# A two-layer transformer on one core: order of two readers of a PSUM bank, key sums, elu minimum, slot numbers and shifts of the plan changed together

## The chip, the cores and the metric

The kernel runs on one core of a Trainium2 chip. A core has a matrix engine (TensorE, here PE, with its weight loads listed apart as PEld), a vector engine (VectorE, DVE), a scalar engine (ScalarE, ACT), a general engine (GpSimd, POOL) and a queue that issues transfers (SyncE, SP). Each has its own stream of instructions, and they meet through semaphores. SBUF is the working memory; PSUM, in eight banks of 128 x 512 numbers here, takes the output of PE, and DVE and ACT read it. The metric is the device time of one execution in microseconds (us); all numbers are float32.

## The reference, cut to what matters

The input is 16 sequences of 256 tokens of width 128. Four blocks follow each other, each with a residual and a LayerNorm:

```python
x = _layernorm(x + L0_attn(x))   # 16 heads of 64, softmax over 256 keys
x = _layernorm(x + L0_ffn(x))    # each token picks one of 64 small splines
x = _layernorm(x + L1_attn(x))   # linear attention and a 65-wide window attention, mixed by a gate
x = _layernorm(x + L1_ffn(x))    # causal attention with normed q and k, then 8 experts of 512
```

Two pieces are touched by the change. In L1_attn the linear attention is

```python
q = jax.nn.elu(q) + 1.0
k = jax.nn.elu(k) + 1.0
kv = jnp.einsum('bsd,bse->bde', k, v)
num = jnp.einsum('bsd,bde->bse', q, kv)
denom = jnp.einsum('bsd,bd->bs', q, k.sum(axis=1))
return num / (denom[..., None] + 1e-06)
```

In L1_ffn the attention divides q and k of each head by their length, `x / sqrt(sum(x * x) + eps)`, before the scores, with 16 heads of 64 and a causal mask over the 256 tokens of a sequence.

## The kernel before, in words

**Groups and stages.** The 4096 tokens are cut into 8 groups of 512 (two sequences, four tiles of 128 tokens). Each group goes through five stages: A (`stage_a`, L773) the first attention, B (`stage_b`, L896) the splines, C (`stage_c`, L1011) linear and window attention, D (`stage_d`, L1241) the causal attention and the gate of the experts, E (`stage_e`, L1398) the experts. Stage D of one group runs while A of a later one and E of an earlier one do, so that PE is fed from several stages.

**The plan.** No stage issues instructions by itself. Each calls `W.add` (L133) with the engine or engines allowed ("VS" is DVE or ACT), a cost in ns, what it reads and writes, a due number, and buffers it must hold. A dependency between two tasks arises only where one of them writes; two readers of the same PSUM buffer are free of each other in the plan. `Plan.order` (L176) takes the due numbers, which are the group's number plus the stage's offset `OFF` (L39) and a fraction within the stage, and adds the random shifts that follow from the seeds in `SHIFTS` (L108). `Plan.line` (L199) then builds one list: again and again it takes the task that could start first by the planned costs, latencies (`LAG`, `OWN`), a price for a change of PE's tiling mode (`DRAIN`, `CHANGE`) and for a change of ACT's function table (`SWITCH`). The engine of a "VS" task, and the slot of each buffer, are settled there too. The list is issued as it stands, so every engine works off its part strictly in that order. Semaphores are put in by the framework afterwards. It also keeps two engines from reading one PSUM bank at once: whichever reader stands second in the list waits for the first, although the plan knows of no such order.

**Slots.** `SLOTS` (L41) gives each class of buffers its number: `ua` (q, k, v of stage A), `uq` and `ud` (q; k and v of stage D), `pb` and `pt` (weights of a softmax before and after transposing), `ov` (attention output), `m`, `k1` (small ones), `c` (stage C), `h2` (stage E's input) and `e` (its sum), and so on. PSUM has four single banks `p` and two double ones `s`.

**The chain of a pair of heads.** `pair` (L635) is used by A and D. PE makes scores into `s`; DVE takes the maximum (L684, or L665 to L680 in D); ACT makes the exponentials and their sums (L703); DVE takes the reciprocal (L710); POOL scales (L716); PE transposes (L731); DVE or ACT copies to `pt` (L583 or L581); PE multiplies by v, and the result is copied to `ov`.

**Ahead of the pairs in D** (`half`, L1251), per half of a sequence's heads: PE projects q into a bank `ps_q`. ACT squares it into `sq` (L1276), and two halves of the same bank are scaled into `uq` by DVE or ACT (L1286 or L1284). PE adds the squares over each head (`hsum`, at L575). k is projected likewise: ACT squares (L1314), DVE or ACT copies the bank to `kn` (L583 or L581), DVE adds the squares (L1318). `rsqrt` (L1225) is a chain of twelve small DVE instructions that ends at L1239. POOL scales `kn` (L1333), PE transposes it (L1343), and the copy `ud` feeds the scores.

**Linear attention in C.** PE projects q into a bank; one reader adds a bias into `ql` (L1031, ACT or DVE), a second one on DVE takes the minimum for elu into `el` (L1032) from the same bank. `outer` (L1065) makes k-transposed times v for a batch with two matmuls of 128 columns, and then the sums of k with two matmuls against a column of ones, `ones1`. The 129 columns are copied to `kv`, and `numer` multiplies q by them.

**The experts in E** (L1398): per expert PE makes four matmuls of 512 columns (`p<-h,w`), ACT a gelu each (L1427), PE sixteen of 128 (`p<-w,hid`), DVE adds with the gate (L1443).

Of the kernel before, what the change touches and what calls it, by code (L numbers as in the profile page):

```python
# [36 lines left out]
NBURST = 2  # L37

OFF = {"a": 0.0, "b": 1.0, "c": 2.0, "d": 3.0, "e": 4.0}  # L39

SLOTS = (  # L41
    ("x", 512, 5),
    ("xT", 512, 1),
    ("ua", 512, 6),
    ("uq", 512, 3),
    ("ud", 512, 5),
    ("pb", 512, 4),
    ("pt", 512, 4),
    ("ov", 256, 7),
    ("m", 64, 30),  # L50
    ("k1", 256, 5),
    ("b", 512, 2),
    ("sc", 288, 1),
    ("c", 512, 7),
    ("qm", 512, 1),
    ("pbC", 512, 3),
    ("ptC", 512, 2),
    ("d", 512, 3),
    ("h2", 512, 2),
    ("kn", 512, 2),  # L60
    ("sq", 512, 2),
    ("e", 512, 2),
    ("hid", 512, 6),
    ("w1", 512, 2),
    ("w2", 512, 2),
# [28 lines left out]
class Plan:  # L94
# [11 lines left out]


    SHIFTS = (  # L108
        258498, 374385, 681190, 1030615, 451157, 416595, 399254, 90386, 402651, 32248, 805286, 535455, 818580,
        975896, 569904, 458668, 418336, 881271, 734960, 774165, 174958, 721137, 512294, 399542, 597858, 678718,  # L110
        303725, 282346, 639604, 797258, 109727, 890232, 734346, 822941, 513168, 691104, 300099, 248650, 750519,
        73556, 12134, 849073, 440403, 472645, 90759, 219759, 480546, 47153, 162702, 851150, 655540, 189313,
        520359, 246779, 231756, 3563, 719028, 365367, 228824, 1016760, 1007179, 536322, 391257, 681015, 841744,
        764356, 292336, 874227, 260578, 294584, 597654, 539960, 432998, 981216, 157434, 356760, 634378, 612323,
        725626, 1029404, 668235, 831714, 603426, 765582, 703452, 266006, 294902, 137908, 1000104, 774373,
        483527, 143664, 261087, 128566, 532895, 360314, 43841, 427189, 701184, 612361, 280258, 1039547, 958460,
        806151, 268661, 680903, 1021345, 131940, 609221, 510023, 159915, 864272, 945906, 103959, 945224,
        853953, 102848, 251619, 243385, 34464, 1011407, 809975, 279597, 61512, 283715, 625865, 369054, 760197,
        54915, 795619, 988242, 350995, 1010712, 973541, 85859, 514023, 986748, 128644, 156637, 776619, 1018136,
        958332, 911372, 562809, 382714, 681013, 1008218, 714451, 7269, 376955, 486985, 122137, 112257, 287473,  # L120
        636101, 931096, 219789, 469256, 840001, 961449, 498852, 1042178, 346761, 224543, 877348, 473884,
        177701, 954649, 151030, 983693, 665266, 779335, 751230, 703298, 614208, 307545,
    )

    def __init__(self, slots):
# [170 lines left out]
def kernel(ctx: ExitStack, tc: tile.TileContext, a: dict, out: bass.AP):  # L296
# [8 lines left out]
    def ctile(name, shape, dtype=F32):  # L305
        return const.tile(shape, dtype, name=name, tag=name)
# [129 lines left out]
    def made(w, cost, fn):  # L436
        W.add("G", cost, fn, w=[w], at=0.4)
# [92 lines left out]

    hsum = ctile("hsum", [P, 2, 32])
    cmask = ctile("cmask", [P, P])
    ones1 = ctile("ones1", [P, 1])

    def setup_consts():
        G = nc.gpsimd
        made(hm, 130, lambda: G.memset(hm, WSCALE))
        for base, sign in ((0, -1), (WD - 1, 1)):
            made(
                hm, 210,  # L540
                lambda base=base, sign=sign: G.affine_select(
                    out=hm, in_=hm, compare_op=ALU.is_ge, fill=0.0, base=base, pattern=[[sign * WD, WH]], channel_multiplier=-sign
                ),
            )
        for i in range(NVM):
            made((ready_c, i), 540, lambda i=i: G.memset(vms[i], 0.0))
        made((ready_c, "o"), 100, lambda: G.memset(ones1, 1.0))
        made((ready_d, "h"), 160, lambda: G.memset(hsum, 0.0))
        for u in range(2):
            for h in range(2):  # L550
                made((ready_d, "h"), 130, lambda u=u, h=h: G.memset(hsum[h * DH : (h + 1) * DH, u, 2 * u + h : 2 * u + h + 1], 1.0))
        made((ready_d, "m"), 600, lambda: make_causal_mask(nc, cmask, NEG))
        made(ready_e, 540, lambda: G.memset(b2blk, 0.0))
        for j in range(NJ):
            W.add("Q", 1000, lambda j=j: nc.sync.dma_start(out=b2blk[j * NE : (j + 1) * NE, j, :], in_=a["L1_ffn_b2"]), w=[ready_e], at=0.5)
# [9 lines left out]
    def dve(n, count=1):  # L565
        return count * (60 + 1.05 * n)

    def scl(n, count=1):
        return count * (60 + 0.84 * n)
# [202 lines left out]

    def stage_a(g):  # L773
        xx = xg[g]
        base = g + OFF["a"]
        W.at = base
        xT = W.buf("xT", "xT")
        transposed(xT, xx, "A")
# [117 lines left out]
    def stage_b(g):  # L896
        xx = xg[g]
        V, G = nc.vector, nc.gpsimd
        base = g + OFF["b"]
        W.at = base  # L900
        xT = W.buf("b", "xTB")
        transposed(xT, xx, "B", after=[end_b])
# [108 lines left out]
    def stage_c(g):  # L1011
        xx = xg[g]
        V, G, A = nc.vector, nc.gpsimd, nc.scalar
        base = g + OFF["c"]
        W.at = base
        nJ = [P, NJ, D]
        xn, hT = W.buf("c", "xnC"), W.buf("c", "hTC")
# [11 lines left out]
        ql, el = W.buf("c", "ql"), W.buf("c", "el")  # L1029
        ps = project(wql, "psql", [ql, el])  # L1030
        W.add("SV", (scl(512), dve(512)), lambda e, ps=ps: act(ql(), ps(), AF.Identity, bias=bql1) if e == "S" else V.tensor_scalar(ql(), ps(), bql1, None, ALU.add), r=[ps], w=[ql])  # L1031
        W.add("V", dve(512), lambda ps=ps: V.tensor_scalar(el(), ps(), bql, 0.0, ALU.add, ALU.min), r=[ps], w=[el])  # L1032
        W.add("S", scl(512), lambda: act(el(), el(), AF.Exp), w=[el], table="exp")
        W.add("V", dve(512), lambda: V.tensor_tensor(out=ql(), in0=ql(), in1=el(), op=ALU.max), r=[el], w=[ql])
        kw, qw = W.buf("c", "kw"), W.buf("c", "qw")
        for dst, w, bias, nm in ((qw, wqw, bqw, "psqw"), (kw, wkw, bkw, "pskw")):
            ps = project(w, nm, [dst])
            W.add("SV", (scl(512), dve(512)), lambda e, ps=ps, dst=dst, bias=bias: act(dst(), ps(), AF.Identity, bias=bias) if e == "S" else V.tensor_scalar(dst(), ps(), bias, None, ALU.add), r=[ps], w=[dst])
        kl, vl, ek = W.buf("c", "kl"), W.buf("c", "vl"), W.buf("c", "ek")
        for j2 in range(2):  # L1040
            ps = W.buf("p", "pslkv")

            def proj(ps=ps, j2=j2):
                for i in range(2):
                    j = 2 * j2 + i
                    mm(ps()[:, i * 2 * D : (i + 1) * 2 * D], hT()[:, j * P : (j + 1) * P], wlkv.rearrange("p c d -> p (c d)"))

            W.add("P", pe(256, count=2), proj, r=[hT], w=[ps], hold=[kl, vl])
            n2 = [P, 2, D]
            half = lambda t, j2=j2: t(J, d=D)[:, 2 * j2 : 2 * j2 + 2, :]  # L1050
            src = lambda c, ps=ps: ps("p (i c d) -> p i c d", i=2, c=2)[:, :, c, :]
            bc = lambda t: t.unsqueeze(1).to_broadcast(n2)
            W.add("V", dve(256), lambda half=half, src=src, bc=bc: V.tensor_tensor(out=half(kl), in0=src(0), in1=bc(bkl1), op=ALU.add), r=[ps], w=[(kl, j2)])
            W.add("V", dve(256), lambda half=half, src=src, bc=bc: V.tensor_tensor(out=half(vl), in0=src(1), in1=bc(bvl), op=ALU.add), r=[ps], w=[(vl, j2)])
        W.add("V", 60 + 0.53 * 512, lambda: V.tensor_scalar(ek(), kl(), -1.0, 0.0, ALU.add, ALU.min), r=[kl], w=[ek])
        W.add("S", scl(512), lambda: act(ek(), ek(), AF.Exp), w=[ek], table="exp")
        W.add("V", dve(512), lambda: V.tensor_tensor(out=kl(), in0=kl(), in1=ek(), op=ALU.max), r=[ek], w=[kl])
# [2 lines left out]
        for b in range(2):  # L1060
# [4 lines left out]
            def outer(b=b, pkv=pkv):  # L1065
                for i in range(2):
                    k = kl(J, d=D)[:, 2 * b + i, :]
                    mm(pkv()[:, :D], k, vl(J, d=D)[:, 2 * b + i, :], start=i == 0, stop=i == 1)
                for i in range(2):
                    k = kl(J, d=D)[:, 2 * b + i, :]  # L1070
                    mm(pkv()[:, D : D + 1], k, ones1, start=i == 0, stop=i == 1)

            W.add("P", pe(P, count=4), outer, r=[kl, vl], w=[pkv], hold=[kv])
            W.add("VS", (dve(129), scl(129)), lambda e, pkv=pkv, kv=kv: copy(e, kv()[:, : D + 1], pkv()[:, : D + 1]), r=[pkv], w=[kv])
            pn, rden = W.buf("p", "pn"), W.buf("m", "rden")

# [164 lines left out]
    def stage_d(g):  # L1241
        xx = xg[g]
        V, G, A = nc.vector, nc.gpsimd, nc.scalar
        base = g + OFF["d"]
        W.at = base
        xn, hT, z = W.buf("d", "xnD"), W.buf("d", "hTD"), W.buf("d", "zD")
        layernorm(xn, xx, "D", [ready_d])
# [3 lines left out]
        def half(b, hf):  # L1251
# [13 lines left out]
            for u in range(2):  # L1265
# [7 lines left out]
                        mm(ps_q()[:, i * S : (i + 1) * S], wqf[:, p * P : (p + 1) * P], hT()[:, b * S : (b + 1) * S])  # L1273

                W.add("P", pe(S, count=2), proj, r=[hT], w=[ps_q], hold=[*sq_qs, qT])
                W.add("S", scl(512), lambda sq_q=sq_q, ps_q=ps_q: act(sq_q(), ps_q(), AF.Square), r=[ps_q], w=[sq_q])  # L1276

                for i in range(2):

# [5 lines left out]
                        else:  # L1285
                            V.tensor_scalar(qT()[:, o], ps_q()[:, o], c, None, ALU.mult)  # L1286

                    W.add("VS", (391, 357), keep, r=[ps_q], w=[(qT, i)])
            pq, nT, pn = W.buf("p", "pq"), W.buf("k1", "nT"), W.buf("p", "pnT")

            def norms():
# [18 lines left out]
            for u in range(2):  # L1310

                ps_k, sq_k, kn = W.buf("p", "psk"), W.buf("sq", "sqk"), kns[u]
                W.add("P", pe(256, count=2), lambda ps_k=ps_k, u=u: by_tokens(ps_k, wkf, cols[u]), r=[hT], w=[ps_k], hold=[sq_k, *kns])
                W.add("S", scl(512), lambda sq_k=sq_k, ps_k=ps_k: act(sq_k(), ps_k(), AF.Square), r=[ps_k], w=[sq_k])  # L1314
                W.add("VS", (dve(512), scl(512)), lambda e, kn=kn, ps_k=ps_k: copy(e, kn(), ps_k()), r=[ps_k], w=[kn])
                W.add(
                    "V", dve(512),
                    lambda sq_k=sq_k, u=u: V.tensor_reduce(  # L1318
# [79 lines left out]
    def stage_e(g):  # L1398
        xx, h2, gate = xg[g], h2Ts[g], gates[g]
        V, G = nc.vector, nc.gpsimd  # L1400
        base = g + OFF["e"]
        W.at = base
        n = NJ * NE
        begun = object()
# [100 lines left out]
```

## Time and profile before

| | us |
|---|---|
| median of 3 runs (lowest to highest) | 2134.72 (2130.21 to 2135.82) |
| the profiled execution: its own time | 2128.94 |
| its span, first to last instruction | 2127.2 |
| PE busy | 2029.2 (95%) |
| DVE busy | 1627.5 (77%) |
| ACT busy | 1296.4 (61%) |
| POOL busy | 901.5 (42%) |

Busy time of PE counts matmuls from start to a modelled end, and one begins before the last has ended; so a PE that waits a little still looks busy. A float32 matmul is two records in the trace, a transpose is one. In the groups of the profile a row names the line, engine and operation, then what is written and read, the number of records, and after the bar the busy time, the mean of one in ns, and the idle time ahead of them with what ended it. In the table of waits a row tells who waited for whom, the total in us, how many times, and the longest.

### The profile page before, as it was taken

The numbers are of one execution on the slowest core, as the hardware profiler recorded it, in microseconds if no ns is written. First come the engines' busy times: TensorE is split into PE (matmuls) and PEld (weight loads), VectorE is DVE, ScalarE is ACT, GpSimd is POOL, SyncE is SP. The second block draws the span as 40 slices with busy tenths as digits, with TensorE's granted clock in tenths as the row PEclk, the third lists the DMA queues.
The fourth block names the chain that finished last, engine by engine and source line by source line (L and its number), as shares of the span: only waits on it lengthen the run. The fifth ranks groups of instructions, "written<-read, shape, count | busy, mean of one in ns | idle before, by whom it ended". The sixth has DMA issues, their size and how long they took to land. (4 is left out here: it accounts for less than half of the span.)

```text
span 2127.2 us, 46285 instructions
## 1 busy us (share of the span) xinstructions
PE 2029.2 (95%) x16458; PEld 1536.6 (72%) x16458; DVE 1627.5 (77%) x4921; ACT 1296.4 (61%) x4249; POOL 901.5 (42%) x1545
## 2 busy tenths in 40 slices
PE   8999999999999999999999999999999899899987
PEld 6777777777777777777777777777767677676755
DVE  6889899998668984799829988498946982994642
ACT  4566767666666664766647657476646664764642
POOL 4445564464235630555406644055613650541321
PEclk9999999999999999999999999999999999999989
DMA  5200000000110001000020000200011002001101
GB/s 134 45 1 2 2 1 2 2 2 1 41 41 11 2 16 50 16 11 2 16 63 13 2 1 16 61 11 2 1 45 36 6 6 75 7 2 50 31 21 50
DMA packets 69529, 47.76 MB, mean 22 GB/s; under 512 B 12113, under 2 KB 59953, under 8 KB 69297
## 3 DMA queue, kind: packets, MB, share of 16 engines
q1 hardware_dynamic: 68720, 43.74, 7.6%
q8 instruction: 131, 2.15, 0.4%
q10 hardware_dynamic: 576, 1.05, 0.2%
q14 instruction: 102, 0.83, 0.1%
HBM read 41.89 MB, written 2.88 MB: 21 GB/s over the span
## 5 line engine op out<-in xcount | busy, mean ns | idle before, releaser
L716 POOL TENSOR_SCALAR pb<-pb,m 128x256 f32<-128x256 f32 (+1 forms) x1024 | 455.1, 462 | 759.5 <-DVE m L710 666.0
L1427 ACT ACTIVATE hid<-p,b 128x512 f32<-128x512 f32 x256 | 172.2, 688 | 292.2 <-PE p L575 287.7
L703 ACT ACTIVATE pb<-s,m 128x256 f32<-128x256 f32 x512 | 238.1, 486 | 90.2 <-DVE m L684 73.3
L703 ACT ACTIVATE pb<-s,m,m 128x128 f32<-128x128 f32 (+1 forms) x512 | 256.3, 521 | 26.9 <-DVE m L680 22.6
L731 PE MATMUL p<-ident,pb 128*128 128x128 f32 x1792 | 262.4, 279 | 10.6 <-POOL pb L716 2.7
L1443 DVE SCALAR_TENSOR_TENSOR e<-p,m,e 128x128 f32<-128x128 f32 x256 | 74.4, 343 | 246.1 <-PE p L575 161.2
L575 PEld LDWEIGHTS p<-w,hid 128*128 128x128 f32 x2048 | 238.3, 192 | 27.9 <-issue 18.2
L731 PEld LDWEIGHTS p<-ident,pb 128*128 128x128 f32 x1792 | 200.6, 141 | 79.5 <-POOL pb L716 34.8
L575 PE MATMUL p<-w,hid 128*128 128x128 f32 x2048 | 241.6, 275 | 5.3 <-DMA w<-in_L_ffn_w_dram 5.0
L575 PE MATMUL p<-h,w 128*128 128x512 f32 x512 | 239.5, 604 | 1.5 <-ACT hid L1427 1.4
L583 DVE COPY pt<-p 128x512 f32<-128x512 f32 (+1 forms) x285 | 170.6, 613 | 23.5 <-PE p L731 22.5
L1165 POOL TENSOR_TENSOR pbC<-pbC,m 128x384 f32<-128x384 f32 (+1 forms) x128 | 119.7, 940 | 160.4 <-DVE m L1161 139.8
L1157 ACT ACTIVATE pbC<-s,m 128x96 f32<-128x96 f32 (+1 forms) x512 | 174.4, 375 | 18.8 <-DVE m L1147 13.0
L684 DVE TENSOR_REDUCE m<-s 128x4 f32<-128x1024 f32 x128 | 153.6, 1213 | 13.2 <-PE s L575 12.9
L575 PEld LDWEIGHTS p<-h,w 128*128 128x128 f32 x512 | 91.4, 191 | 94.7 <-issue 77.4
L581 ACT COPY pt<-p 128x512 f32<-128x512 f32 (+1 forms) x227 | 115.7, 546 | 64.3 <-PE p L731 50.4
L575 PE MATMUL s<-ua,ua 64*128 64x256 f32 x1024 | 137.9, 395 | 3.3 <-ACT pb L703 2.7
L674 DVE TENSOR_REDUCE m<-s 128x2 f32<-128x512 f32 (+1 forms) x256 | 131.5, 545 | 0.8
L575 PE MATMUL p<-pt,ua 128*64 128x256 f32 x1024 | 131.5, 387 | 0.4 <-ACT uq L1284 0.3
L1157 ACT ACTIVATION_READ_ACCUMULATOR pbC<-s,m 128x1 f32 x512 | 116.2, 227 | 0.0
L575 PE MATMUL s<-ud,uq 64*128 64x128 f32 (+1 forms) x1024 | 112.1, 344 | 4.2 <-DVE ud L583 1.4
L575 PEld LDWEIGHTS s<-ua,ua 64*128 64x128 f32 x1024 | 91.0, 187 | 33.6 <-issue 10.5
(271 smaller groups left out, 4334.4 us busy)
## 6 DMA issues: line engine op xcount, KB each, us to landing
w<-in_L_ffn_w_dram SPq DMA_DIRECT2D x128, 256.0 KB, 2.7
x<-_attn_hidden_states_dram SPq DMA_DIRECT2D x8, 256.0 KB, 5.0
out_dram<-x SPq DMA_DIRECT2D x7, 256.0 KB, 2.3
dpad<-k SPq DMA_DIRECT2D x1, 768.0 KB, 10.3
wq<-in_L_attn_Wq_dram ACTq DMA_DIRECT2D x2, 256.0 KB
wkv<-in_L_attn_Wkv_dram ACTq DMA_DIRECT2D x2, 256.0 KB, 5.8
wkv<-in_L_attn_Wkv_dram SPq DMA_DIRECT2D x2, 256.0 KB, 6.4
wo<-in_L_attn_Wo_dram SPq DMA_DIRECT2D x1, 512.0 KB
```

Source lines behind the costliest of these rows:

```text
L575: nc.tensor.matmul(o, lhsT=lhsT, rhs=rhs, start=start, stop=stop)
L581: nc.scalar.copy(o, i)
L583: nc.vector.tensor_copy(o, i)
L674: lambda qc=qc, c0=c0, nk=nk: nc.vector.tensor_reduce(nm()[:, :, qc], sps(S2, a=2)[:, :, c0 : c0 + nk], AX.X, ALU.max, negate=True),
L684: lambda: nc.vector.tensor_reduce(nm(), sps(S2, a=2).rearrange("p a (b k) -> p a b k", k=S), AX.X, ALU.max, negate=True),
L703: act(pb()[:, c0 : c0 + nk], s[:, par, c0 : c0 + nk], AF.Exp, bias=nmx()[:, 2 * par + qc : 2 * par + qc + 1], accum_out=sums()[:, 2 * par ...
L716: eng.tensor_scalar(pb()[:, c0 : c0 + nk], pb()[:, c0 : c0 + nk], sums()[:, 2 * par + qc : 2 * par + qc + 1], 1.0, ALU.mult, ALU.mult,)
L731: nc.tensor.transpose(tps()[:, at * P : (at + 1) * P], pb()[:, c0 + kc * P : c0 + (kc + 1) * P], ident)
L1157: act(pb("p (u k) -> p u k", u=4)[:, u, :nk], s8[:, hp, :nk], AF.Exp, bias=nmx()[:, hp : hp + 1], accum_out=sm()[:, u : u + 1])
L1165: G.tensor_tensor(out=w4, in0=w4, in1=sm()[:, :4].unsqueeze(2).to_broadcast([P, 4, nk]), op=ALU.mult)
L1427: W.add("S", 571, lambda ph=ph, hid=hid, ec=ec: act(hid(), ph(), AF.Gelu_apprx_tanh, bias=b1[:, ec : ec + 1]), r=[ph], w=[hid], table="gel ...
L1443: V.scalar_tensor_tensor(m, pe_()[:, j * D : (j + 1) * D], gate()[:, j * NE + e_ : j * NE + e_ + 1], m, ALU.mult, ALU.add)
```

## The change

Six things are changed.

1. In `half` of stage D a token `squared` is written by each square and read by the scalings of q and by the copy of k. The plan now has the square ahead of the other readers of that bank.
2. In stage C `el` is made from `ql` in SBUF (which already holds the bias plus one, so one is taken away) and no longer from the bank.
3. v of the linear attention gets rows of 129 numbers in a slot class of its own, `vl`; POOL writes ones into the last column (four numbers per partition, once a group), and `outer` makes two matmuls of 129 columns. `ones1` and its two matmuls per batch are gone.
4. Slots: `ua` 6 to 5, `uq` 3 to 4, `ud` 5 to 4, `pb` 4 to 5, `ov` 7 to 9, `m` 30 to 26, `k1` 5 to 7, `sc` 1 to 2, `c` 7 to 6 with one `vl` beside it, `h2` 2 to 1, `e` 2 to 1.
5. All seeds in `SHIFTS` are others, so the order of the whole list is another.
6. Due numbers go through `due(g, stage)` with a factor `PACE`; all its factors are 1.0, so the numbers are the same.

```diff
+PACE = {"a": 1.0, "b": 1.0, "c": 1.0, "d": 1.0, "e": 1.0}
+def due(g, stage):
+    return g * PACE[stage] + OFF[stage]
...
-    ("ua", 512, 6),
-    ("uq", 512, 3),
-    ("ud", 512, 5),
-    ("pb", 512, 4),
+    ("ua", 512, 5),
+    ("uq", 512, 4),
+    ("ud", 512, 4),
+    ("pb", 512, 5),
...
-    ("ov", 256, 7),
-    ("m", 64, 30),
-    ("k1", 256, 5),
+    ("ov", 256, 9),
+    ("m", 64, 26),
+    ("k1", 256, 7),
...
-    ("sc", 288, 1),
-    ("c", 512, 7),
+    ("sc", 288, 2),
+    ("c", 512, 6),
+    ("vl", 516, 1),
...
-    ("h2", 512, 2),
+    ("h2", 512, 1),
...
-    ("e", 512, 2),
+    ("e", 512, 1),
...
     SHIFTS = (
-        258498, 374385, 681190, 1030615, 451157, 416595, 399254, 90386, 402651, 32248, 805286, 535455, 818580,
...
+        622819, 418701, 637725, 96704, 886183, 543474, 823736, 685116, 940842, 108037, 40737, 69874, 1024157,
...
-        made((ready_c, "o"), 100, lambda: G.memset(ones1, 1.0))
...
-        W.add("V", dve(512), lambda ps=ps: V.tensor_scalar(el(), ps(), bql, 0.0, ALU.add, ALU.min), r=[ps], w=[el])
+        W.add("V", 60 + 0.53 * 512, lambda: V.tensor_scalar(el(), ql(), -1.0, 0.0, ALU.add, ALU.min), r=[ql], w=[el])
...
-        kl, vl, ek = W.buf("c", "kl"), W.buf("c", "vl"), W.buf("c", "ek")
+        kl, vl, ek = W.buf("c", "kl"), W.buf("vl", "vl"), W.buf("c", "ek")
+        vl1 = lambda: vl("p (j e) -> p j e", e=D + 1)
+        W.add("G", 100, lambda: G.memset(vl1()[:, :, D : D + 1], 1.0), w=[(vl, 2)])
...
-            W.add("V", dve(256), lambda half=half, src=src, bc=bc: V.tensor_tensor(out=half(vl), in0=src(1), in1=bc(bvl), op=ALU.add), r=[ps], w=[(vl, j2)])
+            W.add("V", dve(256), lambda j2=j2, src=src, bc=bc: V.tensor_tensor(out=vl1()[:, 2 * j2 : 2 * j2 + 2, :D], in0=src(1), in1=bc(bvl), op=ALU.add), r=[ps], w=[(vl, j2)])
...
-                    mm(pkv()[:, :D], k, vl(J, d=D)[:, 2 * b + i, :], start=i == 0, stop=i == 1)
-                for i in range(2):
-                    k = kl(J, d=D)[:, 2 * b + i, :]
-                    mm(pkv()[:, D : D + 1], k, ones1, start=i == 0, stop=i == 1)
-            W.add("P", pe(P, count=4), outer, r=[kl, vl], w=[pkv], hold=[kv])
+                    mm(pkv()[:, : D + 1], k, vl1()[:, 2 * b + i, :], start=i == 0, stop=i == 1)
+            W.add("P", pe(P + 1, count=2), outer, r=[kl, vl], w=[pkv], hold=[kv])
...
-                W.add("S", scl(512), lambda sq_q=sq_q, ps_q=ps_q: act(sq_q(), ps_q(), AF.Square), r=[ps_q], w=[sq_q])
+                squared = object()
+                W.add("S", scl(512), lambda sq_q=sq_q, ps_q=ps_q: act(sq_q(), ps_q(), AF.Square), r=[ps_q], w=[sq_q, squared])
...
-                    W.add("VS", (391, 357), keep, r=[ps_q], w=[(qT, i)])
+                    W.add("VS", (391, 357), keep, r=[ps_q, squared], w=[(qT, i)])
...
-                W.add("S", scl(512), lambda sq_k=sq_k, ps_k=ps_k: act(sq_k(), ps_k(), AF.Square), r=[ps_k], w=[sq_k])
-                W.add("VS", (dve(512), scl(512)), lambda e, kn=kn, ps_k=ps_k: copy(e, kn(), ps_k()), r=[ps_k], w=[kn])
+                squared = object()
+                W.add("S", scl(512), lambda sq_k=sq_k, ps_k=ps_k: act(sq_k(), ps_k(), AF.Square), r=[ps_k], w=[sq_k, squared])
+                W.add("VS", (dve(512), scl(512)), lambda e, kn=kn, ps_k=ps_k: copy(e, kn(), ps_k()), r=[ps_k, squared], w=[kn])
```

## The prediction

> **What bounds the kernel now.** I read the page's first table, then the groups by shape, the table of waits, and PE's own timeline.
>
> ```profile
> PE 2029.2 (95%) x16458; PEld 1536.6 (72%) x16458; DVE 1627.5 (77%) x4921; ACT 1296.4 (61%) x4249; POOL 901.5 (42%) x1545
> ```
>
> PE is the bound. DVE, next, has 500 us to spare, so work moved between DVE and ACT counts only where PE waits for it. The timeline gives the pace of PE when nothing disturbs it.
>
> ```profile
> 1975.49 3.73 PE L575 MATMUL p<-w,hid 128*128 128x128 f32 x32
> 1979.06 1.88 PE L575 MATMUL p<-h,w 128*128 128x512 f32 x4
> ```
>
> The first row is 32 records in 3.73 us. The last one ends 0.27 us after its start, so the pace is (3.73 - 0.27) / 31 = 112 ns a record; likewise 430 ns for 512 columns. Other undisturbed rows give 216 for 256 columns, 109 for a transpose, 108 to 120 for scores in D and A. These paces over all matmuls sum to about 1856 us. The remaining 270 us of the span are head, tail, changes of tiling mode and waits, so "95% busy" hides a good deal of waiting: starts that are over 150 ns later than their group's median sum to 130 us, in 263 places. I then asked who makes PE and the two readers of a bank wait.
>
> ```profile
> ACT c L1031 <- DVE c L1032: 14.1, 5, 3.9
> DVE kn L583 <- ACT sq L1314: 10.6, 11, 3.0
> DVE uq L1286 <- ACT sq L1276: 9.9, 18, 0.8
> ACT sq L1276 <- DVE uq L1286: 4.2, 7, 1.3
> ACT uq L1284 <- DVE uq L1286: 3.9, 7, 1.3
> ...
> PEld p L1343 <- POOL kn L1333: 17.5, 23, 3.1
> PE p L1343 <- POOL kn L1333: 9.5, 12, 2.7
> PEld p L575 <- DVE uq L1286: 4.9, 10, 1.4
> PEld p L575 <- ACT sq L1276: 3.4, 6, 1.2
> PEld p L575 <- DVE kn L583: 2.8, 6, 1.0
> ```
>
> The first five rows are readers of one bank stopping each other: 42.7 us, none of it PE's own, but each stop holds a strict queue and whatever stands behind it. The rest is where it reaches PE: the work ahead of the pairs in D is PE's most frequent late supplier besides the softmax itself.
>
> **The change part by part.** Numbers of instructions are from the built order of both programs.
>
> *Key sums.* 32 matmuls of one column go, two records each: 64. These rows price them (all matmuls against `ones`, then the same with 129 columns).
>
> ```profile
> L575 PE MATMUL p<-ones,c 128*128 128x1 f32 x64 | 8.1, 230 | 0.0
> L575 PE MATMUL p<-k,c 128*128 128x129 f32 x64 | 10.5, 287 | 0.0
> ```
>
> Start to start they take 111 ns, as much as one of 128 columns, since each has its weight load (192 ns, partly beside the last matmul). So 64 x 111 = 7.1 us leave PE itself. The 129th column costs about 1 ns a record: nothing. [...]
>
> POOL's eight memsets of 128x4 are 8 x 0.1 us (the memset of `ones1` took 105 ns); POOL is 42% busy, and its column is wanted only after k's elu, microseconds later. If that cover goes, 0.8 us.
>
> *elu minimum from SBUF.* The nearest row is the same operation on `ek` in SBUF, 442 ns (L1055), against 742 (L1032): 8 x 0.30 = 2.4 us off DVE. It now waits for `ql` (690 on ACT). In exchange the 14.1 us of ACT waiting for DVE go. PE needs `ql` only in `numer`; between the projection and that matmul the new order has at least 9 us of PE work. On PE's path: 0, between -1 and +1.
>
> *Squares first.* In the old list 18 of the 64 q banks had a scaling ahead of the square, and 25 of the 64 k banks the copy to `kn`. In the new one none has. 53 of 64 `kn` copies go to ACT, behind the square on the same engine (18 before); 59 of 128 scalings go to ACT (37 before). The wait doesn't vanish, it becomes known to the plan. What matters is how much PE work stands between a projection and the PE instruction that needs its outcome, priced by the paces above. From the k projection to L1343: under 11 us in 24 of 64 cases before, in 11 after (median 11.7 to 17.6). The path between is the square 0.60, the sum 0.68, the rsqrt chain (2.7 to 11.4 us from first to last instruction), POOL 1.04 for each of two: the shortest cases are the late ones. From the q projection to `hsum`: under 2 us in 18 of 64 before, 4 after, for a square of 0.60 and a bank conflict. From `kT`'s transposing to the scores: under 3 us in 9, now 4.
>
> The waits that reach PE from here: matmul rows alone (L1343 on POOL 9.5; on square, scaling and `kn` copy together about 10) are 20 us. With the weight-load rows (17.5, 4.9, 3.4, 2.8 and smaller) it is about 47 us; these overlap the running matmul in part. Where late cases fall to between a quarter and a half, some 60% of it goes: 12 by the first count, 28 by the second. I take 15, near the matmul rows, since only they show PE idle; bounds 0 and 47. Late next: POOL's L716 before L731, 15 us in 46 short waits, which nothing here shortens (scores to transposes: median PE work 9.0 to 9.4 us in A, 8.3 to 8.5 in D).
>
> One conflict stays outside the plan: the two scalings of one bank on different engines, 19 units of 64 before, 33 after. By the 3.9 us over 7 waits, 14 more are up to 8 us of ACT or DVE; q waits at least 20 us for its scores in 64 of 64 cases, so 0 on PE; uncovered, +8.
>
> *New order and slots.* PE's changes of tiling mode go from 723 to 737. From scores to another kind takes 306 ns at the median and into scores 205, where like follows like in 109: seven more there-and-back are 7 x 0.29 = 2.0 us. ACT gains about 24 us of copies and four table loads (1283 ns each), DVE loses about 25; hidden by 830 us of idle ACT.
>
> The last stretch is worse. Stage D of the last group without any experts' matmul beside it:
>
> ```profile
> 1984.80:2054.00 69.20, 57.28 (x442) 41.63 (x441) 55.02 (x184) 40.81 (x133) 32.75 (x64) 0.94 0.03 9
> ```
>
> It took 69.2 us for 45.8 us of pace, 1.5 to one. In the new order the experts of group 7 (counting from 1) run out sooner: 53.9 us of D stand alone, 8.1 more at a surplus of 0.5: +4 us. With the experts beside it, that work costs little over its pace. `h2` and `e` with one slot each don't add to that: experts of two groups stand together in neither order.
>
> Sum on PE: -7.1 - 15 + 2.0 + 4 = -16 us. The profiled execution took 2128.94, so it would be 2113; that one stood 5.8 below the median of 2134.72. I forecast a median of **2118.6 us**.
>
> All other waits fall anew with the new order: 130 us less the 20 above is 110 us in some 200 places. I have no sign for it; 15 us either way is about one in seven of it.
>
> **The rivals.**
>
> *No change that can be told* (0.3%, 6.4 us, is about what a measurement of this kernel can tell). The waits for `kn` and `hsum` reappear at another bank reader, and only the matmuls' 7.1 is left, less 6 for modes and tail: 2134. [...] For it: only 20 us are PE's own idle time. Against: the shortest covers have grown, which no reappearing wait undoes.
>
> *Slower: ACT becomes late.* 35 `kn` copies (590 ns) and 22 scalings (483) come to ACT in stage D, in the queue that makes the exponentials: 20.7 + 10.6 = 31.3 us. PE waits for these already, as scores need `s` free:
>
> ```profile
> PEld s L575 <- ACT pb L703: 19.2, 47, 2.0
> ```
>
> If every moved instruction delays an exponential on which PE waits, the time is 2118.6 + 31 = 2150. It is slower than before once over half (16 of 31.3) reaches PE, by 0.3% from 22.5. Against it: ACT is 61% busy and its longest idle row is the gelu's wait for PE, 287.7 us; but that lies in E, not in D.
>
> *Much faster.* All 47 us of these waits go, or the new order also trims L716's: 7.1 + 47 - 6 = 48 less, 2087.
>
> **How the numbers follow.** Forecast 0.50 (2118.6, own range 2104 to 2128), much faster 0.16, no change 0.14, ACT late 0.20. The range goes from the much faster case to the slower one's end, 2087 to 2150, and leaves out under 2 in 10. Faster by over 0.3%: 0.66; within: 0.14; slower: 0.20.
>
> **What would show it.** No row for `ones`; two `p<-vl,c` rows of 129 columns, 64 records. `ACT sq <- DVE uq` gone, `DVE kn <- ACT sq` under 3 us, `PEld p <- POOL kn` under 10. PE busy 2010 to 2025. The D-only stretch near the end about 78 us. I am wrong if `PE s <- ACT pb` grows beyond 15 us, or if PE's waits for L716 grow by what `kn` gives back.

## The result, and the profile after

The changed kernel takes 2101.17 us (median of 4 runs, 2098.47 to 2103.09) against 2132.76 for the kernel before on the same chip (4 runs): a ratio of 0.985, with a 95% interval of 0.983 to 0.9871. That is 31.6 us less, where 16 were forecast. Its profiled execution took 2099.62 us with a span of 2097.8, 29.4 less than the span before. In the changed kernel the lines of the helpers and stages quoted here stand 7 lines lower than before, those of stage D 8 to 9 lower: L582 is the former L575, L1284 the former L1276, L1294 the former L1286, L1342 the former L1333 and L1352 the former L1343.

The page's first table of the changed kernel:

```profile
PE 2014.0 (96%) x16394; PEld 1532.6 (73%) x16394; DVE 1608.9 (77%) x4874; ACT 1311.1 (62%) x4300; POOL 904.3 (43%) x1552
```

PE is busy for 15.2 us less, DVE for 18.6 less, ACT for 14.7 more. The next lines are from its table of waits: who waited for whom, us in total, times, the longest.

```profile
PEld p L1352 <- POOL kn L1342: 3.8, 8, 1.0
PE p L1352 <- POOL kn L1342: 1.7, 4, 0.8
DVE uq L1294 <- ACT sq L1284: 3.5, 6, 1.8
DVE uq L1294 <- ACT uq L1292: 10.1, 15, 1.3
ACT uq L1292 <- DVE uq L1294: 2.1, 3, 0.9
PEld s L582 <- ACT pb L710: 15.8, 54, 1.2
```

The reader is to see three things. PE's waits for `kn` are down from 17.5 and 9.5 us to 3.8 and 1.7. DVE stands for squares 3.5 us where it stood 20.5 (9.9 and 10.6). And the conflict that the plan still doesn't know, between the two scalings of one bank, has grown from 3.9 to 12.2. The row of `elu`, 14.1 us of ACT waiting for DVE on a bank, is gone; what that is worth in time no run shows apart.

The key sums' matmuls as a group by shape, and as a window the stretch at the end in which stage D of the last group is without experts (its bounds, its length, the busy time and instructions of PE, PEld, DVE, ACT and POOL, then the granted clock):

```profile
L582 PE MATMUL p<-vl,c 128*128 128x129 f32 x64 | 9.8, 287 | 0.0
```

```profile
1952.50:2024.70 72.20, 63.01 (x521) 47.85 (x519) 62.07 (x206) 49.68 (x165) 37.27 (x77) 0.96 0.03 9
```

**Where the 29 us came from.** I took every matmul's start to the next one's in groups by line, names and shape, and called late what exceeds its group's median by over 150 ns, where the profile names an engine or a transfer that ended the wait. Late starts sum to 122.8 us in 235 places before, 100.8 in 198 after: 22.0 less. (The prediction's 130 us in 263 places is the same kind of count; how the groups are drawn moves it by some us.) Those ended by the work ahead of the pairs in D (`kn` on POOL, square, scaling, copy to `kn`) fell from 27.9 to 6.9, by 21.0: `kn` on POOL 12.2 to 2.6, scalings on DVE and ACT 7.8 to 1.0, squares 5.2 to 0.6, while the copy stayed at 2.7. All others sum to 1.0 less, with both signs among them: `pt` on DVE -6.6, the small buffers `k` on DVE +7.6. The matmuls of the key sums and of k times v take 9.7 us where they took 14.9 (7.1 for the one-column ones, 7.8 for the others): 5.2 less, or 5.6 without the late starts among them, which are counted already. That leaves 1.8 of 29.4.

### The profile page after: what moved, and what is told of

It reads as the page before. It is cut to its first block, busy times and chain, and to the rows that moved or that the text cites. A ratio compares the mean times of both kernels' runs of the same rounds, so it can differ in the third digit from the quotient of the medians.

```text
span 2097.8 us, 46229 instructions
## 1 busy us (share of the span) xinstructions
PE 2014.0 (96%) x16394; PEld 1532.6 (73%) x16394; DVE 1608.9 (77%) x4874; ACT 1311.1 (62%) x4300; POOL 904.3 (43%) x1552
## 4 chain that ended last, share of the span: by engine, by line
PE 55%; DVE 34%; ACT 4%; POOL 4%; issue 3%; DMA 0%; POOLq 0%; DVEq 0%; ACTq 0%
PE p L582 40%; PE s L582 6%; PE p L738 5%; DVE m L681 3%; DVE m L691 3%; DVE pt L590 2%; DVE s L672 2%; DVE s L1149 2%; ACT pb L710 2%; POOL pb L723 2%; DVE m L1154 2%; DVE m L604 2%; PE p L1178 1%; DVE x L620 1%; DVE d L620 1%
## 5 line engine op out<-in xcount | busy, mean ns | idle before, releaser
L582 PEld LDWEIGHTS p<-w,hid 128*128 128x128 f32 x2048 | 237.9, 192 | 24.1 <-issue 17.1
L582 PE MATMUL p<-w,hid 128*128 128x128 f32 x2048 | 240.8, 276 | 2.9 <-DMA w<-in_L_ffn_w_dram 2.6
L582 PE MATMUL p<-h,w 128*128 128x512 f32 x512 | 242.1, 609 | 0.4 <-DVE kn L590 0.3
L582 PEld LDWEIGHTS p<-h,w 128*128 128x128 f32 x512 | 92.4, 193 | 95.7 <-issue 78.4
L582 PE MATMUL s<-ua,ua 64*128 64x256 f32 x1024 | 137.5, 394 | 1.3 <-ACT pb L710 0.8
L582 PE MATMUL p<-pt,ua 128*64 128x256 f32 x1024 | 132.6, 387 | 0.5 <-DVE pt L590 0.5
L681 DVE TENSOR_REDUCE m<-s 128x2 f32<-128x256 f32 (+1 forms) x256 | 131.1, 547 | 0.8
L582 PE MATMUL s<-ud,uq 64*128 64x128 f32 (+1 forms) x1024 | 114.1, 346 | 1.0 <-ACT pb L710 0.4
L582 PEld LDWEIGHTS s<-ua,ua 64*128 64x128 f32 x1024 | 91.0, 186 | 29.5 <-issue 8.1
```

The lines of the kernel that those rows point to most:

```text
L582: nc.tensor.matmul(o, lhsT=lhsT, rhs=rhs, start=start, stop=stop)
L681: lambda qc=qc, c0=c0, nk=nk: nc.vector.tensor_reduce(nm()[:, :, qc], sps(S2, a=2)[:, :, c0 : c0 + nk], AX.X, ALU.max, negate=True),
```

## The experiments

In the first seven runs, the order of tasks on every engine is that of the kernel named, since only what a task does is edited, not what the plan knows of it. In the others the plan is made anew. The runs were made on several chips, each with runs of the kernel before beside them (medians of 2130.21 to 2133.01 us); so two rows are best compared by their ratios.

| run | us | ratio to before (95%) |
|---|---|---|
| e1 before, `kn` not waiting | 2146.27 | 1.0076 (1.0055 to 1.0097) |
| e2 changed, `kn` not waiting | 2108.88 | 0.990 (0.9881 to 0.9918) |
| e3 before, squares off the bank | 2116.64 | 0.9932 (0.9914 to 0.9951) |
| e4 changed, squares off the bank | 2098.52 | 0.9856 (0.9831 to 0.988) |
| e5 changed, one-column matmuls back | 2106.77 | 0.9886 (0.9871 to 0.9901) |
| e6 before, half an rsqrt | 2114.92 | 0.9924 (0.9903 to 0.9944) |
| e7 changed, half an rsqrt | 2083.84 | 0.9779 (0.9762 to 0.9795) |
| e8 before, token | 2204.08 | 1.0346 (1.033 to 1.0361) |
| e9 before, no shifts | 2179.95 | 1.0232 (1.0217 to 1.0248) |
| e10 before, token, no shifts | 2184.94 | 1.026 (1.0243 to 1.0277) |
| e11 changed, no shifts | 2168.30 | 1.0181 (1.0166 to 1.0196) |
| e12 changed, no token, no shifts | 2156.95 | 1.0126 (1.0111 to 1.0141) |
| e13 changed, no token, new seeds | 2121.63 | 0.9951 (0.9935 to 0.9967) |
| e14 the same, second seeds | 2131.16 | 1.0001 (0.9991 to 1.001) |
| e15 before, token, new seeds | 2124.00 | 0.9966 (0.9955 to 0.9977) |
| e16 changed, new seeds | 2112.65 | 0.9906 (0.9886 to 0.9925) |
| e17 changed, seeds searched further, two Newton steps | 2088.47 | 0.9798 (0.9783 to 0.9812) |
| e18 as e17 with three steps | 2098.72 | 0.9842 (0.9826 to 0.9859) |

### Is it the work ahead of the pairs? (e1 to e4)

Theory one: the gain came from that work. Theory two: it came from the new seeds, anywhere in the list.

```diff
-                        in1=rqk()[:, 16 + 8 * u : 24 + 8 * u].unsqueeze(2).to_broadcast([P, 8, DH]), op=ALU.mult,
+                        in1=hm8.unsqueeze(2).to_broadcast([P, 8, DH]), op=ALU.mult,
```

> The kernel before with its own order on every engine; the scaling of kn on POOL (L1333) multiplies by a constant, so it no longer waits for the rsqrt chain (L1239). Left out: the division of k by its length. Theory one (the gain came from the work ahead of the pairs in D): PE's matmuls at L1343 start 9.5 us late on POOL, their weight loads 17.5, so the time falls by 10 to 18 us, to 2115 to 2123. Theory two (the gain came from the new seeds, anywhere): under 6 us, since the next late supplier takes over.

> The changed kernel, same edit, same order. Theory one: what this wait cost is already gone (1.7 us of PE's matmuls wait for POOL's kn), so the time falls by 0 to 4 us, to 2097 to 2101. Theory two: it falls by as much as the same edit gives the kernel before, within 3 us.

Both theories missed: the kernel before became 15 us slower, the changed one some 8 by the medians and 11 by the ratios. The wait itself fell by more than half. Groups of the kernel before first, then waits and groups of e1:

```profile
L1237 DVE TENSOR_TENSOR m<-m 128x32 f32<-128x32 f32 x96 | 24.2, 252 | 0.8
L1238 DVE SCALAR_TENSOR_TENSOR m<-m,m 128x32 f32<-128x32 f32 x96 | 24.2, 252 | 0.9
L1239 DVE SCALAR_TENSOR_TENSOR m<-m,m 128x32 f32<-128x32 f32 x96 | 22.5, 234 | 0.6
```

```profile
PEld p L1343 <- POOL kn L1333: 7.2, 9, 3.1
PE p L1343 <- POOL kn L1333: 4.6, 5, 2.7
```

```profile
L1237 DVE TENSOR_TENSOR m<-m 128x32 f32<-128x32 f32 x96 | 26.7, 278 | 0.8
L1238 DVE SCALAR_TENSOR_TENSOR m<-m,m 128x32 f32<-128x32 f32 x96 | 27.8, 290 | 0.9
L1239 DVE SCALAR_TENSOR_TENSOR m<-m,m 128x32 f32<-128x32 f32 x96 | 27.7, 289 | 0.6
```

The second number after the first bar is the mean of one in ns: the same chain instructions take up to 55 ns more. POOL's `kn` now runs beside the rsqrt chain (14.1 us of overlap with these three lines, 0 before), and the exponentials still wait for the chain. So the edit put one delay in place of another, and says nothing on the theories; it did show the longer DVE instructions told of at the end. DVE is busy 13.7 us longer, and PE runs 55.6 us at half its clock (31.8 before); how the 15 us divide between the two isn't shown.

The next edit makes both squares read 512 columns of `wq` in SBUF; of each line only the call is shown:

```diff
...
-act(sq_q(), ps_q(), AF.Square)
+act(sq_q(), wq[:, :512], AF.Square)
...
-act(sq_k(), ps_k(), AF.Square)
+act(sq_k(), wq[:, :512], AF.Square)
...
```

> The kernel before with its own order; both squares in D read 512 columns of wq in SBUF and not the bank, so no two engines read that bank except the two scalings. Left out: the true lengths of q and k. Theory one: PE's long waits for square, scaling and kn copy (5.2, 5.8 and 2.7 us over the pace) go and DVE is not stopped for 20 us, so the time falls by 8 to 18 us, to 2115 to 2125. Theory two: under 5 us.

> The changed kernel, same edit, same order. Theory one: 0 to 4 us less, 2097 to 2101, since the plan already put the readers apart. Theory two: as much as the edit gives the kernel before, within 3 us.

Theory one as expected: 14 us in the kernel before (2130.89 to 2116.64); in the changed one 2.7 by the medians, which are from two chips, and nothing by the ratios (0.985 and 0.9856). With the order of every engine unchanged, the readers' conflicts were worth about 14 us, and the new order has rid itself of all or nearly all of them. In e3 every wait of DVE for a square has left the table, while `kn` on POOL keeps its waits:

```profile
PEld p L1343 <- POOL kn L1333: 17.2, 22, 2.6
PE p L1343 <- POOL kn L1333: 9.0, 12, 2.2
```

The edit also frees the square from waiting for the projection; that this alone gains little is what e4 shows. So some 12 us (medians) to 16 us (ratios) of the 31.6 come from readers of these banks; by the intervals of the ratios it is 8 either way.

### The key sums by themselves (e5)

```diff
                     mm(pkv()[:, : D + 1], k, vl1()[:, 2 * b + i, :], start=i == 0, stop=i == 1)
+                for i in range(2):
+                    k = kl(J, d=D)[:, 2 * b + i, :]
+                    mm(pkv()[:, 256:257], k, vl1()[:, 2 * b + i, D : D + 1], start=i == 0, stop=i == 1)
```

> The changed kernel with its own order; after the two matmuls of 129 columns per batch come two of one column again, with the ones from the last column of vl, into an unused column of the same bank. By the spacing in the trace of before (111 ns a record, 64 records) the time rises by 7.1 us over the changed kernel, to 2108. [...]

The medians differ by 5.6 us; the difference of the ratios, 0.0036, is 7.7, and from their intervals it is 5 either way. In the trace of e5, start to start, the 64 records take 7.5 us, 117 ns each (one late start of 1.1 us among them; the median is 112). Together with the 129-column ones they take 15.7 us, where the changed kernel's take 9.7:

```profile
L582 PE MATMUL p<-vl,c 128*128 128x1 f32 x64 | 8.4, 235 | 0.0
```

So a one-column matmul is priced by the spacing measured: 117 ns here and 111 in the kernel before, as much as one of 128 columns (112). Each of the 64 in the kernel before had a weight load of 192 ns; that the load is the reason for the spacing is argued, not shown.

### Is `kn` the reason, or DVE's load? (e6, e7)

```diff
+        each_ = each
         for k in range(3):
             src, dst = (y, o) if k % 2 == 0 else (o, y)
+            each = each_ if k == 0 else (lambda fn, r, w: each_(lambda: None, r, w))
...
```

> The kernel before with its own order; two of three Newton steps of the rsqrt are left out (6 of 12 small DVE instructions), so L1239 comes some 1.5 us or more sooner and POOL still starts kn after the chain, not within it. Left out: accuracy of the lengths. If late kn and late lengths held PE (12.1 us over the pace at L1343), the time falls by 8 to 16 us, to 2115 to 2123. If DVE's own load mattered no more than elsewhere and kn was covered: under 4 us.

> The changed kernel, same edit, same order. If the plan has already covered kn: 0 to 5 us less than the changed kernel, 2096 to 2101. If the same relief of DVE helps both alike, as much as in the kernel before within 3 us.

The kernel before gains 16.6 us, as the first answer had it; but the changed kernel gains 17.3, as the second had it, though hardly any `kn` is late in it. In the kernel before the late starts for `kn` fall from 12.2 to 3.5; in the changed one from 2.6 to 0, with 4.4 off the small buffers `k` on DVE, 2.1 off `ud`, 1.6 off the softmax weights. DVE's busy time falls by 28.2 us in the one and 27.8 in the other. Here is the page's first table of e7:

```profile
PE 2009.6 (97%) x16394; PEld 1530.6 (74%) x16394; DVE 1581.1 (76%) x4682; ACT 1309.7 (63%) x4300; POOL 904.2 (43%) x1552
```

By the ratios the changed kernel gains 15. A microsecond off DVE in this place was worth about 0.6 us of time in both kernels, at 77% busy. It isn't shown apart whether that is the load or the chain's place before the exponentials.

### Token or search? (e8 to e12)

The token `squared` alone, on the kernel before, with its own seeds:

```diff
-                W.add("S", scl(512), lambda sq_q=sq_q, ps_q=ps_q: act(sq_q(), ps_q(), AF.Square), r=[ps_q], w=[sq_q])
+                squared = object()
+                W.add("S", scl(512), lambda sq_q=sq_q, ps_q=ps_q: act(sq_q(), ps_q(), AF.Square), r=[ps_q], w=[sq_q, squared])
...
-                    W.add("VS", (391, 357), keep, r=[ps_q], w=[(qT, i)])
+                    W.add("VS", (391, 357), keep, r=[ps_q, squared], w=[(qT, i)])
...
```

> The kernel before with the token squared alone; seeds, slots and the rest as before, so the whole order falls anew. If planning the two readers is what pays, the waits between the readers of these banks (DVE on square 20.5 us, square on DVE 4.2) go under 8 us, and the time falls by 8 to 20 us, to 2111 to 2123, give or take what a new order does by itself. If only the search pays, the seeds no longer fit this plan and the time is 2131 or more.

The waits for squares did fall (1.7 us on DVE), and yet the time rose by 73 us: seeds found for one plan were worth nothing on this other one (2204.08 with them, 2184.94 without any in e10). So single parts can't be compared under seeds that were found for something else. The next four have no shifts at all, with and without the token:

```diff
-        for seed in self.SHIFTS:
+        for seed in ():
```

> The kernel before with no shifts: every task at the due number that its stage and its remaining path give. By e8, where the seeds no longer fitted the plan, a list without fitting seeds costs some 70 us: 2190 to 2215.

> The kernel before with the token squared and no shifts. If planning the two readers pays by itself: 8 to 20 us less than the kernel before without shifts. If it only gives the search a truer plan: the same within 5 us, and any order by itself can be 5 off.

> The changed kernel with no shifts. If parts 1 to 4 (tokens, elu, key sums, slots) carry the 31 us: 20 to 35 us less than the kernel before without shifts. If the search carries it: 0 to 12 us less, about the key sums' 7.

> The changed kernel without the token squared and no shifts. If planning the two readers pays: 8 to 20 us more than the changed kernel without shifts. If not: within 5 us of it.

Without a search the token doesn't pay: 5.0 us slower on the kernel before, 11.4 slower on the changed one, where both my answers missed. (e9, with 2179.95, came out under the 2190 to 2215 that I expected.) The other parts (elu, key sums, slots) gain 23 us without token and shifts (2179.95 to 2156.95), but each of these is one draw of an order. The shifts are worth 50 us on the kernel before (2179.95 to 2130) and 67 on the changed one (2168.30 to 2101; another chip). Of my answers, "the search carries it" held for the token and the bound of 0 to 12 us for e11 (11.7).

### Does the search carry over better with the token? (e13 to e16)

New seeds were found by hill climbing: draw a seed, keep it if the plan gets shorter by its own costs, and stop where the plan is as long as that of the kernel it stands beside.

```diff
     SHIFTS = (
-        622819, 418701, 637725, 96704, 886183, 543474, 823736, 685116, 940842, 108037, 40737, 69874, 1024157,
...
```

> The changed kernel without the token squared; other seeds, found by the same hill climb on this plan until it is as long by the plan's own costs as the changed kernel's (within 0.3 us). If knowing the order of the readers makes the search carry over: the waits between square and scaling or copy come back (over 15 us on DVE and ACT) and the time is 8 to 20 us above the changed kernel, 2109 to 2121. If any search does as well: 2096 to 2106.

> The same with a second, independent set of seeds of the same planned length. The two differ by what a search leaves to chance: I expect under 8 us. Same two answers as for the run before.

> The kernel before with the token squared alone (its own slots, elu and key sums), seeds searched to a planned length within 1.1 us of the kernel before's. If the token makes the search carry over: 10 to 20 us below the kernel before, 2111 to 2121. If not: 2126 to 2136.

> The changed kernel with all its parts and an independent set of seeds of the same planned length (within 0.1 us). If the changed kernel's time is what this plan gives and not luck: 2095 to 2108. If its seeds were a lucky draw: over 2110.

At one planned length, the changed kernel without the token takes 2121.63 and 2131.16 on the chip, with it 2101.17 and 2112.65. The means are 19.5 us apart, and two draws of one kind differ by 9.5 and 11.5, more than the 8 that I expected. So a plan of one length seems worth more on the chip when it knows the order of the readers. Four draws suggest it and don't prove it, and one rival is left: all were stopped at one planned length, not after one effort. A plan without the token has fewer orders to keep, so the same effort may have made it shorter. e13 and e14 lie above the ranges that I had written for them, and e16 came out over 2110, as I had said for the case that the changed kernel's seeds were a lucky draw. Waits of e13, then of e14, both without the token (the lines of e14 stand 4 lower in number):

```profile
DVE kn L590 <- ACT sq L1323: 9.7, 12, 1.5
DVE uq L1294 <- ACT sq L1284: 5.8, 11, 1.3
ACT uq L1292 <- DVE uq L1294: 5.5, 8, 1.5
ACT sq L1323 <- DVE kn L590: 5.0, 8, 2.1
ACT sq L1284 <- DVE uq L1294: 2.5, 3, 1.1
```

```profile
DVE uq L1290 <- ACT sq L1280: 8.4, 11, 1.3
ACT sq L1319 <- DVE kn L586: 6.5, 7, 2.7
ACT sq L1280 <- DVE uq L1290: 2.9, 4, 1.2
```

The waits that the token keeps out are back, 23.0 us between square, copy and scaling in e13 (9.7, 5.8, 5.0, 2.5) and 17.8 in e14, where the changed kernel has 3.5 and e16 2.5. That the token removes these waits is shown; how much time that gives apart from the draw is not. On the kernel before, e15, the token gains 6.2 us where I expected 10 to 20, between my two answers; there PE waits for `kn` in 5.2 us of matmul rows again, so this draw may have lost elsewhere what it gained here.

### What the runs point to (e17, e18)

Seeds of the changed kernel, searched on, and one Newton step fewer:

```diff
...
+        each_ = each
         for k in range(3):
-            src, dst = (y, o) if k % 2 == 0 else (o, y)
...
+            src, dst = ((y, y), (y, o), (y, o))[k]
+            each = each_ if k < 2 else (lambda fn, r, w: each_(lambda: None, r, w))
...
```

> The changed kernel with its seeds searched further (the plan is 8.4 us shorter by its own costs) and two Newton steps in the rsqrt in place of three (9 of 12 small DVE instructions; the outcome stays a float32 root to some millionths). If DVE's load is what the chain costs: half of the 17 us of the shorter chain, so 8 below the run beside it. If the seeds carry over as far as those of the changed kernel: 2084 to 2096 in all.

> The same seeds with all three Newton steps. If a shorter plan carries over: 2092 to 2100, 1 to 9 below the changed kernel. If two searches of the same length already differ by 11 us on the chip, anything from 2090 to 2110 can come out.

The plan of e18 is 8.4 us shorter by its own costs; the chip gives 2.5 (2098.72), less than two draws differ. The Newton step left out gives 10.2 us, 17.0 off DVE's busy time, again 0.6 to one. e17 is faster than both kernels: 2088.47 us, a ratio of 0.9798. Only e7 is faster, 2083.84, with a rougher root.

## Why the prediction was wrong

*The direction, and the place, held.* PE's waits for `kn`, square and scaling went, as the counts of PE work between producer and consumer had it (those for the copy stayed at 2.7 us), and most marks were met: `ACT sq <- DVE uq` is gone, `DVE kn <- ACT sq` too, `PEld p <- POOL kn` is 3.8 where under 10 was named, PE is busy 2014.0 us. One was missed: the D-only stretch took 72.2 us where about 78 was named. The time fell below the forecast's own range of 2104 to 2128, towards the case that had 0.16. The mechanism was right, and two terms of the sum had the wrong size.

*The step that failed most* is the term for the last stretch: "8.1 more at a surplus of 0.5: +4 us". It took for granted that the stretch would go on costing 1.5 times its work. The stretch grew by 3.0 us only (69.2 to 72.2) for 8.1 us more work, and by the term's own paces the surplus over the work fell from 69.2 - 45.8 = 23.4 us to 72.2 - 53.9 = 18.3: 5.1 less, where 4 more was forecast. Its late starts (as counted above) fell from 16.7 to 11.0 us, most of it softmax weights: those ended by POOL's scaling from 3.7 to 0.3, by DVE's copy `pt` from 2.5 to 0.4. The prediction had looked at how much work stands there, not at what that work waits for. That it was the new order that shortened these waits, and what in it, no run shows.

*The second* is "I take 15, near the matmul rows, since only they show PE idle; bounds 0 and 47". It measured 21.0. The matmul rows (20 us) understated what was there, since a matmul that starts late may still begin before the modelled end of the last one; late starts against the group's median give 27.9 us for the same suppliers, and they were part of the 130 us quoted at the prediction's start. And I let 60% of it go; 75% went.

In the prediction's terms the span's 29.4 us are then 21.0 for the waits, 5.1 for the last stretch and 5.6 for the key sums, less 2.3 for all the rest. The first two overlap by less than 1 us: of the waits ahead of the pairs, 0.8 us stood in that stretch before and 1.6 after.

*Key sums:* forecast 7.1 us. One-column matmuls did take 7.1 in the trace of before and 7.5 when put back, so the spacing held; both sums hold late starts. "The 129th column costs about 1 ns" held too: the median spacing is 113 ns where it was 112. Without late starts the trace shows 5.6 less, e5 5.6 to 7.7.

*Modes:* the +2 can't be read apart. *Two scalings of one bank:* up to 8 us more of ACT or DVE was said, and 8.3 came.

*Waits elsewhere:* "I have no sign for it" was right in sum, 1.0 us, with single suppliers moving by 8 either way. *ACT late* didn't come: `PEld s <- ACT pb` fell from 19.2 to 15.8 with 14.7 us more on ACT.

*"DVE, next, has 500 us to spare, so work moved between DVE and ACT counts only where PE waits for it"* was too easy. e6, e7 and e17 against e18 show about 0.6 us of time for each us off this DVE chain in stage D. The changed kernel has 18.6 off DVE; that this, by its copies of `kn` gone to ACT, is part of why the waits fell further than I took is argued, not shown.

*What the forecast couldn't know* is the draw. e13 to e16 put two searches of the same length 9 to 12 us apart, and the seeds of the changed kernel beat mine by 11.5. A gain of 16 and one of 31 are hard to tell apart in advance if the order is one draw of many. How much of the 31.6 is draw stays open; readers (e3 less e4) some 12 to 16 and key sums 5 to 8 are what fixed orders show, each some us either way. What `elu` and the slots gave by themselves, no run shows.

## What to carry to other kernels

When a planner lays out a tuned list, put into it every order that the framework will force anyway: a search can exploit whatever the plan doesn't know, and then the chip gives it back. (Here two draws each stood 19.5 us apart at the same planned length, which suggests it; the waits themselves, 23.0 and 17.8 us against 3.5 and 2.5, are shown.) A part of such a change can't be judged by adding it under seeds that were tuned for another plan (73 us too slow in e8); either keep the list and edit what the tasks do, or search again on both sides, twice. And price waits of a pipelined engine by late starts against the group's usual spacing, not by the idle time that the page names, and look in every stretch for what it waits for, not only for how much work it has.

## What the runs showed of the hardware

**DVE's instructions on SBUF took longer beside POOL.** In the trace of the kernel before, DVE's 128x32 instructions of the rsqrt chain (L1237) take a mean of 181 ns with POOL idle and 298 beside it (POOL busy for at least 95% of the instruction; 45 and 30 of them); 128x4 products (L680) 150 and 530 (92 and 29); scalings of 128x128 from SBUF (L613) 338 and 452 (90 and 91). Copies from PSUM took the same either way: 683 and 678 for 512 columns (141 and 111). Part of the excess is a matter of choice, since an instruction that waits for POOL falls into POOL's time by that; but in e1, where the same chain got POOL's `kn` beside it, its means rose by 26 to 55 ns. L1237 and L680 read two tensors from SBUF, L613 one; what holds DVE up there, no run shows.

**The granted clock was halved for a few us at a time, often after little work of PE.** The records of the granted clock show stretches at 0.5. In the kernel before they begin at 1035.95, 1694.72, 2046.29 and 2117.97 us and last 3.41, 3.41, 13.65 and 11.27 us; in the changed one four last 3.41, one 10.24 and the last 12.15. So each is a multiple of 3.413 us, but for the last of a trace, in which PE has nothing left to do. They sum to 31.8 us in the kernel before and 36.0 in the changed one, but 100.2 in e8 (mean granted clock 0.993, 0.992 and 0.978), and in each of these traces they begin whole multiples of 3.413 us apart (193, 103 and 21 of them in the kernel before). Of the 15 ahead of the last in e8, 12 follow 3.4 us in which PE was busy for less than half the time; in the kernel before it is 2 of 3 (36% and 29%), in the changed one 3 of 5 (42, 35 and 19%). Little work isn't all of it: the one at 1036 us in the kernel before follows 3.4 us with PE busy for 97%. The PE timeline of e8, with the idle time before a row and what ended it in brackets, and a window over the same place, whose granted clock is the 0.66 near its end:

```profile
1575.14 0.60 PE L1345 MATMUL p<-ident,kn 128*128 128x128 f32 x4
...
1584.50 0.45 PE L627 MATMUL p<-ident,d 128*128 128x128 f32 x1 [3.04 <-DVE d L613]
1585.66 0.95 PE L627 MATMUL p<-ident,d 128*128 128x128 f32 x3 [0.71 <-DVE d L613]
...
1601.32 2.07 PE L575 MATMUL p<-h,w 128*128 128x512 f32 x2
```

```profile
1580.00:1610.00 30.00, 24.24 (x157) 15.41 (x155) 20.65 (x77) 17.32 (x58) 11.76 (x18) 0.66 0.04 10
```

The clock is halved from 1583.54 us, within the wait of 3.04 us, to 1604.02, and in that time two matmuls of 512 columns take 2.07 us where two took 1.02 in the kernel before. Half speed for 68 us more than before is up to 34 of e8's 73 us, as an estimate. In the 3.4 us ahead of this stretch PE was busy for 38%. So 20.5 us at half the clock began within a wait of PE of 3.04 us; whether the wait brought them, and what it cost beyond its length, no run shows.
